# Splitting the bias rows of a graph network's first layer, moving query rows to GpSimd, and a new instruction order for the first block

## The chip, the cores and the metric

One NeuronCore of a Trainium2 chip runs the whole kernel in one launch. The metric is the device time of one execution in microseconds (us); several runs are given by their median. The engines are TensorE (PE), VectorE (DVE), ScalarE (ACT), GpSimd (POOL) and SyncE (SP). Each works through its own instruction queue in order; an instruction waits for semaphores of other engines or of transfers (DMA).

## The reference, cut

Four graph layers run over 4096 nodes with 64 features and a 0/1 adjacency matrix `adj` of 4096 x 4096. The change touches only the first:

```python
h = relu(layernorm(x))
h = lorentz_linear(h, W, b, scale)        # x @ W.T + b, then a time column and a rescaled rest
q = lorentz_linear(h, Wq, bq, scale_q)
k = lorentz_linear(h, Wk, bk, scale_k)
att = sigmoid((2 + 2 * (qm @ k.T)) / att_scale + att_bias)   # qm: q with the time column negated
support = (adj * att) @ h
x = x + support / sqrt(|-support[:, 0]**2 + sum(support[:, 1:]**2)|)
# layers 2 to 4: a decayed sum over the last 100 neighbours, a sum A @ h, a mean over neighbours
```

`lorentz_linear` gives `time = sigmoid(h[:, 0]) * exp(scale) + 1.1` as the first column and `h[:, 1:] * sqrt((time**2 - 1) / sum(h[:, 1:]**2))` as the rest.

## The kernel before, in words

**Blocks and masks.** Nodes are 32 tiles of 128 rows, eight blocks of four tiles. For each block of 512 targets the adjacency comes in 16 pieces of 128 x 2 x 512 (`load_masks`, L226, a DMA on POOL's queue that turns f32 into fp8), 128 pieces in all, block 7 first. Eight semaphores serve these loads in turn, so a load waits until the one eight before it has landed. `todo` lists the pieces in order. The masks of four blocks (64 pieces) have room from the start; the other four share room with the prologue's tiles (`pro`), and are opened after `pro_stack.close()`.

**The prologue** (`first_rows_and_block`, `before0`) makes h, q and k for two groups of 16 tiles, tiles 16 to 31 first. For each group: layer norm on DVE and ACT (`st`, `xc`, `sq`, `va`, `rs`), transposes on PE (`pt_h`), copies by ACT (`ht`), a product with W (`ps_h`; L719 adds the bias by a product of `ones` with `brow`, L727 multiplies by the weights), copies by ACT (`t`), the sigmoid and squares (`sgh`, `sqh`), sums and roots on DVE (`rrh`, `t2h`), the rows `fb` on DVE with their time column on POOL (L854); then the same for queries and keys together: `pt_q`, `hq`, `ps_q`, `tq`, `sqq`, `rrq`. Keys (`kr`) are made by DVE, with the time column by POOL (L903). Queries go to `s2a` (the same room as `q_sb`; L892, L903): those of tiles 16 to 31 by DVE, those of tiles 0 to 15 by POOL. Keys are transposed (`pt_k`) and laid by ACT as `kt`, queries of a block (`pq`, L989) as `qt`.

**Bias rows.** `bias_rows` (L501 to L510, POOL) splits the three bias vectors, 192 columns, into three bf16 parts that add up, and puts them into rows 0 to 2 of each half of `brow`. Twelve POOL operations do it.

**The first block.** The scores of block 7 (`ps`, L1053) need `kt` and `qt`; ACT takes the sigmoid into `att`, DVE multiplies by the mask, and PE gathers with `fb` (`acc`, L1084). Six `att` tiles and three score places rotate. All steps of prologue, block 7 and two pieces of block 6 are parts of a `Listing`, each with an engine and a planned time; `run` emits them by the list of numbers `ORDER`, taking the first part that can go. The first 40 mask loads are parts too. While PE has nothing planned, `fill` puts in products of `ones` (`idle`, L1178), 43 at the start and then planned idle time divided by 0.215.

**The loop.** The other pieces go in rounds of up to four: scores, sigmoid, mask, one mask load each (`load_masks(1)`), then gathers of the round before. `queries(ib - 1)` transposes the next block's queries, `rows0` finishes a block's rows (POOL's `sup`, `rs_a` and others). From the 33rd piece on, DVE also checks pieces of the adjacency (`ck`, loaded by SP).

The functions that the diff touches:

Of the kernel before, what the change touches and what calls it, by code (L numbers as in the profile page):

```python
# [24 lines left out]
D = 64  # L25
P = 128
# [17 lines left out]


ORDER = (
    206, 207, 205, 209, 208, 203, 210, 0, 1, 2, 3, 5, 4, 7, 9, 6, 8, 10, 213, 64, 11, 12, 14, 15,
    204, 13, 16, 18, 17, 211, 216, 65, 66, 67, 68, 69, 70, 19, 71, 217, 20, 21, 72, 214, 73, 127,
    74, 75, 76, 22, 79, 24, 23, 212, 215, 26, 218, 77, 78, 81, 25, 27, 28, 219, 80, 83, 82, 84,
    29, 31, 30, 85, 87, 33, 34, 32, 86, 221, 89, 88, 35, 36, 220, 37, 38, 90, 91, 222, 39, 40, 92,  # L50
    41, 43, 93, 94, 45, 96, 95, 97, 44, 223, 98, 47, 49, 100, 224, 46, 225, 42, 99, 102, 48, 101,
    50, 51, 52, 53, 60, 103, 104, 106, 56, 108, 110, 54, 57, 128, 105, 55, 61, 107, 129, 109, 111,
    62, 133, 228, 63, 161, 112, 113, 134, 149, 226, 114, 162, 230, 121, 115, 130, 150, 145, 146,
    163, 157, 151, 116, 131, 153, 119, 137, 138, 123, 124, 232, 135, 132, 164, 152, 120, 139, 158,
    136, 122, 154, 169, 147, 233, 173, 155, 170, 177, 174, 229, 165, 117, 231, 234, 156, 166, 58,
    59, 148, 159, 160, 167, 118, 235, 178, 140, 179, 236, 237, 125, 141, 126, 189, 193, 171, 142,
    143, 181, 238, 190, 185, 239, 172, 186, 191, 192, 144, 175, 176, 187, 241, 194, 195, 200, 182,
    201, 197, 240, 180, 198, 183, 184, 202, 242, 199, 196, 188, 227, 168,
)


# [32 lines left out]
def kernel(  # L94
# [87 lines left out]
    def model(general):  # L182
# [7 lines left out]
        def pool(name, bufs, on=stack, **kw):  # L190
            return on.enter_context(tc.tile_pool(name=name + sfx, bufs=bufs, **kw))
# [284 lines left out]
        pro = pool("pro", 1, pro_stack, side="right")  # L476
        pa0 = pool("pa0", 1, l0, space=PSUM)
        pps = [pool(f"pp{n}", 1, l0, space=PSUM) for n in range(2)]
        ppro = pool("pp_p", 1, pro_stack, space=PSUM)
        w_sb = pro.tile([P, NW], F32, name="w_sb" + sfx)  # L480
        weights_in(w_sb)
        for gr in range(1, len(ROWS)):
# [7 lines left out]
        ones = pro.tile([P, P], BF16, name="ones" + sfx)  # L490
        dve.memset(ones, 1.0)

        def bias_rows():
            v = vec[:, V_B : V_B + 3 * D]
            sel = pro.tile([P, 3], F32, name="sel" + sfx)
            high = pro.tile([P, 3 * D], BF16, name="high" + sfx)
            left, part = (
                pro.tile([P, 3 * D], F32, name=f"brow_{a}{sfx}") for a in ("left", "part")
            )
            total = pro.tile([P, 3 * D], F32, name="brow_sum" + sfx)  # L500
            nc.gpsimd.tensor_tensor(sel, ident[:, 0:3], ident[:, D : D + 3], ALU.add)  # L501
            for n in range(3):
                nc.gpsimd.tensor_copy(high, v if n == 0 else left)
                to = total if n == 0 else part
                nc.gpsimd.tensor_scalar(to, high, sel[:, n : n + 1], None, ALU.mult)
                if n:
                    nc.gpsimd.tensor_tensor(total, total, part, ALU.add)
                if n < 2:
                    nc.gpsimd.tensor_tensor(left, v if n == 0 else left, high, ALU.subtract)
            nc.gpsimd.tensor_copy(brow, total)  # L510

        class Listing:

# [10 lines left out]
            def add(self, engine, us, emit, *after, takes=(), frees=None, at=0.0, form=None):  # L524
                part = SimpleNamespace(
                    engine=engine, us=us, emit=emit, after=after, takes=takes, frees=frees, at=at,
                    form=form, n=len(self.parts), then=[], place=None,
                )
                for q in after:
                    q.then.append(part)  # L530
                self.parts.append(part)
                return part
# [49 lines left out]
                dve.scalar_tensor_tensor(q, q, share, a, ALU.mult, ALU.mult)  # L582
                dve.tensor_tensor(to, q, z, ALU.add)

        tables, flats = [], []

        TURN = ("pm", "pa")

# [1 line left out]
            on, tag = (pm, "pr") if part.place == "pm" else (pa0, "pa")  # L590
            return on.tile(list(shape), F32, tag=tag, name=name + sfx)

        def before0(todo, gr, bias):

            v = SimpleNamespace(at={})
            r0, R = ROWS[gr]
# [4 lines left out]
            def add(engine, us, emit, *after, **kw):  # L601
                return todo.add(engine, us, emit, *after, **kw)
# [132 lines left out]
            for u in HALF:  # L735
                pairs = [(k, k) for k in range(u * HK, (u + 1) * HK)]
                hs.append(
                    add(
                        "PE", 1.3 if u == 0 else 1.05, product("ht", pairs, 1, W_L, u == 0, "h"), ht[u], *hs, bias,
                        **({"takes": ("ps", "pp1")} if u == 0 else {}),  # L740
                    )
                )
# [123 lines left out]

            def q_out(u):
                def emit(_):
                    if u == 0:
                        v.tq = buffer("C", "tq", [P, len(HALF), 2, 2 * HK, D])  # L870
                    act.copy(v.tq[:, u].rearrange("p s k d -> p s (k d)"), v.at[f"q{u}"])
                return emit

            for u in HALF:
                pairs = [(k, u * HK + k) for k in range(HK)]
                qs.append(
                    add(
                        "PE", 1.3, product("hq", pairs, 2, W_QK, True, f"q{u}"), hq[u],
                        takes=("ps", "pp1"),
                    )  # L880
                )
                tq.append(add("ACT", 1.02, q_out(u), qs[u], frees=qs[u]))
# [29 lines left out]
                kr.append(add("DVE", 0.65, qk_rows(u, 1, nc.vector), rq, *kr))  # L912
                krw.append(add("POOL", 0.3, qk_times(u, 1), kr[u]))
            for u in reversed(HALF):
                if lead:
                    q = add("DVE", 0.65, qk_rows(u, 0, nc.vector), rq)
                else:
                    q = add("POOL", 1.35, qk_rows(u, 0, nc.gpsimd), rq)
                fq[u] = add("POOL", 0.3, qk_times(u, 0), q)
            ktd = across(lambda u: v.kr[:, of(u), :], "k", [[x] for x in krw], None)  # L920
            return hw, fq, ktd

# [166 lines left out]
        def first_rows_and_block():  # L1089
# [1 line left out]

            listing = Listing()
            add = listing.add
            bias = add("POOL", 8.1, lambda _: bias_rows(), at=6.5)
            made = [before0(listing, gr, bias) for gr in range(len(ROWS))]

            table = add("ACT", 1.5, lambda _: act.activation(tried, tried, AF.Sigmoid), *tables)
            for part in flats:
# [88 lines left out]

        with tc.manual_schedule():
            acc, late = first_rows_and_block()
            push(rows0(order0[0], evacuated(order0[0], acc, 0)), 10)  # L1190
            pro_stack.close()
            mp1 = pool("mask_b", 1, side="right")
            for ib in order0[EARLY:]:
                get_mask(mp1, ib)
            pps.append(pool("pp2", 1, l0, space=PSUM))
            if not general:
                push(count_constants(), 1)
            asking = iter(())

            def on():  # L1200
                step()
                next(asking, None)

            sizes = [2] * 8 if general else [4] * 4
            first = [2] * 7 if general else [4, 4, 3, 3]
            sizes = first + (NIB - 2) * sizes + [0]
            k, done = NG + 2, NG
            LEAVING = {112 - 4 * ib: ib for ib in range(NIB)}  # L1210
            for size in sizes:
                now = []
                for n, (ib, g) in enumerate(todo[k : k + size]):
                    edge[0] = n == size - 1
                    ps = scores(ib, g)

                    if size > 2 and not now:
                        att = frm = sigmoids(ps, att_tile(ib, g))
                    else:
                        frm, att = sigmoids(ps), att_tile(ib, g)  # L1220
                    masked(ib, g, frm, att)
                    now.append((ib, g, att))
                    load_masks(1)
                    k += 1
                    if k == 92 and not general:
                        push(count_constants_2(), 1)
                    if not general and k in LEAVING:
                        taken(LEAVING[k])
                    if k > 2 * NG and k % 8 in (0, 2, 4, 5, 7):
                        check()  # L1230
                    on()
                for ib, g, att in late:
                    at = done % NG
                    if at == 0:
                        acc = pa0.tile([P, IB], F32, tag="pa", name=f"acc0_{ib}{sfx}")
                        if ib > 0:
                            asking = queries(ib - 1)
                    gather(acc, fb, g, att, at)
                    if at == NG - 1:
                        push(rows0(ib, evacuated(ib, acc, 0)), 10)  # L1240
                    done += 1
                late = now
            edge[0] = True
            if len(checks) % 2:
                check()
            if general:
                drain()
# [659 lines left out]
```

## Time and profile before

| | us |
|---|---|
| median of 3 runs | 569.07 |
| lowest, highest | 568.34, 570.71 |
| the profiled execution | 568.73 |
| its span | 567.0 |
| PE busy | 544.4 |
| DVE busy | 468.2 |
| ACT busy | 357.1 |
| POOL busy | 280.2 |

The span runs from the first to the last instruction that the profile shows. PE's busy time holds its filler matmuls. The chain of waits follows the work that ended last back through what released it; in a line of it the first number is the start, the second the duration. In the windows each row is a stretch of time with the busy time of each engine (and the count of its instructions), the granted TensorE clock as a share of full speed, the share of time that the DMA engines were busy, and GB/s.

### The profile page before, as it was taken

What the parts mean: (1) busy time and instruction counts of PE and PEld (TensorE: products, weight loads), DVE (VectorE), ACT (ScalarE), POOL (GpSimd) and SP (SyncE); (2) the same over time, 40 slices, a digit from 0 to 9 for tenths busy, and PEclk for the clock granted to TensorE, in tenths of its full rate; (3) what the DMA queues carried; (4) which work ended last, traced back from release to release, by engine and by line L of the source; (5) the groups of instructions that cost most, each with busy time, mean ns of one, the idle gap of its engine ahead of it and who ended that gap; (6) DMA issues with size and microseconds to landing.
All of it is one profiled execution on the core that took longest, in us unless ns stands there. A gap on an engine that the chain in (4) does not pass through costs nothing.

```text
span 567.0 us, 9853 instructions
## 1 busy us (share of the span) xinstructions
PE 544.4 (96%) x3335; PEld 279.5 (49%) x3335; DVE 468.2 (83%) x949; ACT 357.1 (63%) x651; POOL 280.2 (49%) x538
## 2 busy tenths in 40 slices
PE   8898999999999999999999999999999999999995
PEld 3553333333333333332334445445454888888884
DVE  5788866899998999898965977778969897789992
ACT  3589577667766758778632888988888332342231
POOL 8626614666867575754345400475644442234332
PEclk9899999999999999999999999999999999999998
DMA  8983992798999999993234255443534778859960
GB/s 141 146 82 32 86 96 20 84 145 142 166 153 148 170 151 172 130 156 97 92 123 136 102 201 163 141 153 116 173 125 149 251 266 294 281 173 328 353 242 21
DMA packets 45612, 87.86 MB, mean 155 GB/s; under 512 B 6272, under 2 KB 24576, under 8 KB 45552
## 3 DMA queue, kind: packets, MB, share of 16 engines
q1 hardware_dynamic: 26112, 69.14, 36.3%
q0 software_dynamic: 18912, 17.77, 33.5%
q8 instruction: 28, 0.46, 0.3%
q10 hardware_dynamic: 528, 0.23, 0.2%
q14 instruction: 32, 0.26, 0.1%
HBM read 135.60 MB, written 1.05 MB: 241 GB/s over the span
## 4 chain that ended last, share of the span: by engine, by line
PE 63%; DVE 14%; POOL 8%; DMA 7%; ACT 4%; issue 3%; SPq 0%; ACTq 0%; DVEq 0%; POOLq 0%
PE acc L1627 15%; PE acc L1084 13%; PE ps L1053 12%; PE acc L1530 8%; PE cnt L1495 8%; DVE att L88 4%; DMA mask<-adjt_dram 3%; DVE ckw L88 2%; POOL mask L226 2%; PE many L1382 1%; DMA s2a<-adjt_dram 1%; DVE s2a L88 1%; PE idle L1178 1%; DMA vec<-vecs_dram 1%; ACT w L88 1%
## 5 line engine op out<-in xcount | busy, mean ns | idle before, releaser
L1053 PE MATMUL ps<-qt,kt 64*128 64x512 f32 x512 | 122.3, 608 | 3.6 <-DVE att L88 3.3
L1084 PE MATMUL acc<-att,fb 128*64 128x512 f32 x512 | 117.1, 599 | 0.5 <-DVE att L88 0.5
L1627 PE MATMUL acc<-s,mask 128*128 128x256 f16 x1024 | 114.0, 273 | 0.4 <-DVE s L88 0.4
L88 ACT ACTIVATE w<-cnt 128x512 int16<-128x512 f32 x187 | 98.7, 606 | 13.0 <-PE cnt L1495 12.1
L1627 PEld LDWEIGHTS <-mask 128*128 128x128 fp8e4 x1024 | 99.8, 98 | 12.9 <-issue 1.0
L88 DVE TENSOR_TENSOR att<-ps,mask 128x1024 f32<-128x1024 f32 x82 | 98.6, 1218 | 9.1 <-ACT ps L88 8.9
L88 DVE SCALAR_TENSOR_TENSOR ckw<-ckw 128x1024 f32<-128x1024 f32 x76 | 96.0, 1273 | 4.0 <-DMA ckw<-adjt_dram 4.0
L88 ACT ACTIVATE ps<-ps,att_c,att_a 128x1024 f32<-128x1024 f32 x82 | 93.8, 1176 | 1.1 <-PE ps L1053 0.7
L88 ACT ACTIVATE att<-ps,att_c,att_a 128x1024 f32<-128x1024 f32 x46 | 54.4, 1203 | 53.0 <-PE ps L1053 48.6
L1053 PEld LDWEIGHTS ps<-qt,kt 64*128 64x128 f32 x512 | 46.1, 186 | 77.5 <-issue 30.2
L226 POOL DMA_DIRECT2D mask<-adjt_dram x128 | 70.3, 562 | 11.0 <-DMA mask<-adjt_dram 9.5
L1495 PE MATMUL cnt<-mask,after 128*128 128x512 fp8e4 x256 | 67.4, 379 | 3.6 <-DMA mask<-two 1.3
L88 DVE TENSOR_TENSOR att<-att,mask 128x1024 f32<-128x1024 f32 x46 | 57.2, 1263 | 14.6 <-ACT att L88 11.2
L1084 PEld LDWEIGHTS acc<-att,fb 128*64 128x64 f32 x512 | 33.8, 136 | 71.6 <-issue 68.4
L1530 PE MATMUL acc<-w,s2a 128*128 128x512 bf16 x256 | 66.2, 379 | 1.2 <-ACT asb L88 1.2
L88 DVE TENSOR_SCALAR w<-cnt 128x512 int16<-128x512 f32 x69 | 46.9, 686 | 23.2 <-PE cnt L1495 22.6
L316 POOL TENSOR_TENSOR rs_a<-rs_y 128x4 f32<-128x4 f32 x48 | 19.1, 398 | 67.6 <-DVE rs_y L88 61.1
L88 DVE SCALAR_TENSOR_TENSOR ck<-ck 128x512 f32<-128x512 f32 x60 | 42.8, 714 | 0.8 <-DMA ck<-adjt_dram 0.8
L1530 PEld LDWEIGHTS <-s2a 128*128 128x128 f16 x256 | 24.7, 98 | 33.6 <-issue 5.6
L88 ACT ACTIVATE xm<-xm,inn 128x64 f32<-128x64 f32 x32 | 10.4, 347 | 47.3 <-DVE high L88 45.1
L1495 PEld LDWEIGHTS <-after 128*128 128x128 bf16 x256 | 24.5, 99 | 31.8 <-issue 2.7
L88 DVE SCALAR_TENSOR_TENSOR s2a<-s2a 128x1024 f32<-128x1024 f32 x22 | 27.7, 1268 | 1.8 <-DMA s2a<-adjt_dram 1.8
(248 smaller groups left out, 611.3 us busy)
## 6 DMA issues: line engine op xcount, KB each, us to landing
ckw<-adjt_dram SPq DMA_DIRECT2D x76, 512.0 KB, 4.4
mask<-adjt_dram POOLq DMA_DIRECT2D x128, 128.0 KB, 8.6
ck<-adjt_dram SPq DMA_DIRECT2D x60, 256.0 KB, 6.0
s2a<-adjt_dram SPq DMA_DIRECT2D x22, 512.0 KB, 4.9
x_sb<-x_dram SPq DMA_DIRECT2D x4, 256.0 KB, 7.5
out_dram<-y POOLq DMA_DIRECT2D x15, 64.0 KB, 3.7
apart_m<-mask SPq DMA_DIRECT2D x16, 16.0 KB, 4.5
mask<-apart_m SPq DMA_DIRECT2D x16, 16.0 KB, 4.7
```

Of the source, the lines that this page charges most:

```text
L88: return op(out, *args, **kw)
L226: nc.gpsimd.dma_start(out=masks[ib][:, g * CG : (g + 1) * CG, :], in_=adjt[ib, g])
L316: nc.gpsimd.tensor_tensor(a, y, y, ALU.mult)
L1053: nc.tensor.matmul(ps[:, c, :], kt[half, g, :], qts[ib][half, :], start=True, stop=True)
L1084: nc.tensor.matmul(acc[c * D : (c + 1) * D, :], lhs[:, t, :], rhs[:, c, :], start=(at == 0), stop=(at == NG - 1), skip_group_check=True,)
L1178: nc.tensor.matmul(v.idle[:, v.filling % CG, :], ones, ones.unsqueeze(1).to_broadcast([P, IB // P, P]), start=True, stop=True, skip_group_ ...
L1382: nc.tensor.matmul(pc[q * NT : (q + 1) * NT, :], lane[:, NT - 1 - t : 2 * NT - 1 - t], masks[quad * QUAD + q][:, t, :], start=(t == 0), st ...
L1495: nc.tensor.matmul(cnt, by, what, start=True, stop=True, skip_group_check=True)
L1530: nc.tensor.matmul(accs[ib], apart_s if t < 0 else both(s2a, t), w, start=(t == NT - 1), stop=False, skip_group_check=True,)
L1627: nc.tensor.matmul(acc[:, to, :, :].rearrange("p k d -> p (k d)"), masks[ib][:, t, c * P : (c + 1) * P], s23[:, t, :, :].rearrange("p k d ...
```

## The change

1. `bias_rows` takes a range of columns. The first 64 (for the product with W) are made first, as a part of its own planned at 3.8 us; the other 128 (for queries and keys) are a second part planned at 6.2 us, on which the products `ps_q` now depend. In the new order POOL issues eight mask loads before the first part (seven before the single one until now) and five between the parts.
2. Blocks 7 and 6 need only the queries of tiles 24 to 31. DVE makes these as before. The other three sets of eight tiles are put into `queries_left`, and POOL makes one (a product and a time write) after each of the first three mask loads of the loop.
3. The prologue's room is given back, and the tiles of the later masks opened, after the last of those; the score place of the prologue is given back before the loop, as before.
4. `ORDER` is a new list. By it PE gets 11, 7, 5, 10, 2, 13 and 1 fillers where it had 14, 5, 5, 10, 2, 13 and 1 (after the 43 at the start). DVE masks seven pieces before its second product `kr` of the second group (six before), and ACT does the last `sqq` before its second copy to `kt` (after it before).

```diff
 ORDER = (
-    206, 207, 205, 209, 208, 203, 210, 0, 1, 2, 3, 5, 4, 7, 9, 6, 8, 10, 213, 64, 11, 12, 14, 15,
...
+    202, 201, 204, 199, 203, 200, 205, 198, 0, 2, 3, 4, 6, 8, 208, 5, 7, 10, 9, 207, 63, 206, 209,
...
-        ppro = pool("pp_p", 1, pro_stack, space=PSUM)
+        ps_stack = ExitStack()
+        ppro = pool("pp_p", 1, ps_stack, space=PSUM)
...
-        def bias_rows():
-            v = vec[:, V_B : V_B + 3 * D]
-            sel = pro.tile([P, 3], F32, name="sel" + sfx)
-            high = pro.tile([P, 3 * D], BF16, name="high" + sfx)
+        sel = pro.tile([P, 3], F32, name="sel" + sfx)
+
+        def bias_rows(c0, n):
+            cols = slice(c0, c0 + n)
+            v = vec[:, V_B + c0 : V_B + c0 + n]
+            high = pro.tile([P, n], BF16, name=f"high{c0}{sfx}")
...
-            nc.gpsimd.tensor_tensor(sel, ident[:, 0:3], ident[:, D : D + 3], ALU.add)
+            if c0 == 0:
+                nc.gpsimd.tensor_tensor(sel, ident[:, 0:3], ident[:, D : D + 3], ALU.add)
...
-            nc.gpsimd.tensor_copy(brow, total)
+            nc.gpsimd.tensor_copy(brow[:, cols], total)
...
-        tables, flats = [], []
+        tables, flats, queries_left = [], [], deque()
...
-                        "PE", 1.3 if u == 0 else 1.05, product("ht", pairs, 1, W_L, u == 0, "h"), ht[u], *hs, bias,
+                        "PE", 1.3 if u == 0 else 1.05, product("ht", pairs, 1, W_L, u == 0, "h"), ht[u], *hs, bias_h,
...
-                        "PE", 1.3, product("hq", pairs, 2, W_QK, True, f"q{u}"), hq[u],
+                        "PE", 1.3, product("hq", pairs, 2, W_QK, True, f"q{u}"), hq[u], bias_qk,
...
             for u in reversed(HALF):
-                if lead:
+                if lead and u == HALF[-1]:
                     q = add("DVE", 0.65, qk_rows(u, 0, nc.vector), rq)
+                    fq[u] = add("POOL", 0.3, qk_times(u, 0), q)
                 else:
-                    q = add("POOL", 1.35, qk_rows(u, 0, nc.gpsimd), rq)
-                fq[u] = add("POOL", 0.3, qk_times(u, 0), q)
+                    queries_left.append((qk_rows(u, 0, nc.gpsimd), qk_times(u, 0)))
...
-            bias = add("POOL", 8.1, lambda _: bias_rows(), at=6.5)
-            made = [before0(listing, gr, bias) for gr in range(len(ROWS))]
+            bias_h = add("POOL", 3.8, lambda _: bias_rows(0, D), at=7.2)
+            bias_qk = add("POOL", 6.2, lambda _: bias_rows(D, 2 * D), at=7.2)
+            made = [before0(listing, gr, bias_h, bias_qk) for gr in range(len(ROWS))]
...
-            pro_stack.close()
-            mp1 = pool("mask_b", 1, side="right")
-            for ib in order0[EARLY:]:
-                get_mask(mp1, ib)
+            ps_stack.close()
             pps.append(pool("pp2", 1, l0, space=PSUM))
...
                     load_masks(1)
                     k += 1
+                    if queries_left:
+                        for emit in queries_left.popleft():
+                            emit(None)
+                        if not queries_left:
+                            pro_stack.close()
+                            mp1 = pool("mask_b", 1, side="right")
+                            for later_ib in order0[EARLY:]:
+                                get_mask(mp1, later_ib)
```

## The prediction

> **What bounds the kernel now.** I read the page first, then the chain of waits over the first 60 us, then the engines' timelines and short windows there, since all that the change moves lies in that stretch or just behind it.
>
> ```profile
> span 567.0 us, 9853 instructions
> PE 544.4 (96%) x3335; PEld 279.5 (49%) x3335; DVE 468.2 (83%) x949; ACT 357.1 (63%) x651; POOL 280.2 (49%) x538
> ```
>
> TensorE (PE) is busy 96% of the span, but in the first 45 us much of that is filler (the `idle` matmuls). Real work of the attention layer begins with the scores at 44.88. In windows from 56.76 to 77.00 PE has no gap, and from 77 to 107 one of 0.21 us. So a gain is worth what it moves the moment from which PE is full of scores and gathers; later work shifts with it.
>
> The chain of waits, cut to the stretch from 0 to 60 us (start, duration, what), gives the way there:
>
> ```profile
> 0.79 6.43 DMA vec<-vecs_dram
> ...
> 15.35 0.70 POOL brow L510
> 16.05 0.04 issue
> 16.09 0.39 PE ps_h L719 x2
> 16.48 1.88 PE ps_h L727 x32
> 18.37 4.61 PE idle L1178 x14
> 22.98 0.87 PE pt_h L678 x8
> ```
>
> The biases land at 7.22; GpSimd (POOL) works on all 192 columns of their rows until 16.05, and PE's first product waits for that. Then the chain runs through 14 filler matmuls: the normalised rows are ready at 21.3, but PE reaches their transposes only at 22.82. The windows show why the fillers are slow (columns: PE, PEld, DVE, ACT, POOL busy, then the granted clock, DMA share, GB/s):
>
> ```profile
> 17.00:18.00 1.00, 1.00 (x22) 1.00 (x20) 0.91 (x2) 0.25 (x1) 1.00 (x3) 0.97 1.09 258
> 18.00:19.00 1.00, 1.00 (x6) 0.46 (x5) 0.00 (x0) 0.60 (x2) 1.00 (x3) 0.50 1.08 252
> 20.00:21.00 1.00, 1.00 (x4) 0.42 (x3) 1.00 (x2) 0.99 (x2) 0.53 (x1) 0.50 1.06 107
> ```
>
> The granted clock is 0.50 from 18 to 21, after a hole (12.36 to 16.09) in which PE did only 1.17 us of transposes.
>
> From 50 us on VectorE (DVE) leads. POOL's timeline there:
>
> ```profile
> 49.94 1.55 POOL L892 TENSOR_TENSOR s2a<-tq,rrq 128x512 f32<-128x512 f32 x1 [4.97 <-ACT att L88]
> 52.64 1.98 POOL L892 TENSOR_TENSOR s2a<-tq,rrq 128x512 f32<-128x512 f32 x1
> ```
>
> and the windows beside it:
>
> ```profile
> 50.00:52.72 2.72, 2.11 (x10) 0.57 (x8) 2.72 (x3) 2.66 (x6) 2.72 (x3) 1.00 0.01 3
> 52.72:56.76 4.04, 3.53 (x17) 1.10 (x17) 4.04 (x4) 3.48 (x4) 4.01 (x4) 1.00 0.20 14
> 56.76:64.60 7.84, 7.84 (x40) 2.97 (x38) 6.52 (x8) 4.60 (x4) 6.48 (x13) 1.00 0.95 79
> ```
>
> DVE has no pause from 50.00 to 56.76, and PE lacks 0.61 and 0.51 us there. Of the maskings (`att<-att,mask`, 1.21 us each) the two that start beside these POOL products, at 50.50 and 53.63, took 2.07. The chain names a mask transfer landing at 50.13 as releaser of the first; DVE was busy with `kr` until 50.50 anyway, so I don't count it.
>
> **The change, step by step.** All against the profiled execution, 568.73 us (span 567.0 and 1.73 around it), 0.34 below the median of 569.07.
>
> *1. Bias rows of 64 columns first.* The same 11 operations took 8.77 us (7.28 to 16.05) at 192 columns. A POOL product of 128x4 takes 0.20, so 11 of them with gaps of 0.06 bound it at 2.9 from below, the old 8.8 from above. A product of 192 columns takes 0.54, which gives 0.31 at 64; casts and scalings by the same share make about 4.5: ready at 11.8. PE ends the transposes at 14.75, so any cost under 7.5 is hidden. The first product begins at 14.78 instead of 16.09, ends near 17.1 instead of 18.37. ScalarE (ACT) is busy with `sq` until 17.25, so its copies `t` move from 18.40 to 17.25: 1.15 gained there.
>
> *2. Fillers 11 instead of 14, later 7 instead of 5.* In other places 13 take 2.98 and 10 take 2.33, 0.23 each. At full clock the 11 end at 19.65. DVE, freed 1.15 earlier by ACT's `rs`, has the second half of `xc` ready at 20.15, PE transposes it until 20.7. ACT finishes `sqh` at 21.2 (22.35 less 1.15) and copies `ht` from there instead of from 23.89. PE's 7 fillers end at 22.3, bias products 0.35, and the first `ps_h` product of the second group starts at 22.65 instead of 25.26: 2.6 gained. That needs the full clock. The hole in PE's matmuls shrinks to 12.36 to 14.78, and in the 3 us before 17.95 PE gets 1.3 us more work than before, so I take it; with 0.50 the fillers end at 21.0, the transposes at 22.05, the product at 24.05: 1.2 gained.
> The Trainium skill ("TensorE: Matmul & The Clock Gate", What's actually happening) says that half rate follows an idle window of some 3.4 us, on windows that run free of the kernel. The old hole is 3.7 us and the trace agrees; the new one of 2.4 can't hold such a window, so by that rule the 2.6 stands.
>
> *3. The other 128 columns, on POOL.* Before them stand five mask loads, each waiting for the landing of the load eight before it; the fifth of those landed at 4.2 + 11.9 = 16.1, so the work starts near 16.9. At 128 columns it costs between 2.9 and 8.8; 6.5 by columns gives 23.4. Four more loads of 0.55 follow (the one they wait for last landed at 16.6 + 6.6 = 23.2), to 25.6, and then `fb`'s time copies, 0.4 each, which PE's transposes `pt_q` want at 26.4. It is hidden by 0.4 only; at 8.8 the copies come 2.3 later (first at 28.3) and eat most of step 2. The products that need these columns start after the transposes and are safe.
>
> *4. To the first scores.* From `pt_q` to `kr` order and counts stay, so all shifts by 2.6; a load put between `fb`'s two last copies delays a half that is needed 0.5 us later: nothing. Scores begin at 42.3.
>
> *5. DVE's busy stretch.* ACT does the last `sqq` before a copy of `kt`: DVE's last reduction, which waited for it until 46.39, comes 0.5 earlier. The two POOL products leave this stretch (2 x 0.86 on DVE), `kr`'s time is written by POOL at once instead of behind a 1.55 product, and one `s2a` product of 0.68 leaves DVE. That outweighs what PE lacked, 0.61 + 0.51 = 1.12, which caps the gain; seven maskings now precede DVE's second `kr`, and gathers of 0.92 follow maskings of 1.21, so some 0.2 stays: 0.9 gained, 0 to 1.12.
>
> *6. Queries in the first round.* Three POOL products with their three time writes now stand behind the 41st, 42nd and 43rd mask load, beside the last maskings of block 7. By landings of 1.25 us each that is about 65 to 73. Queued behind them are mask loads needed 20 tiles later and `sup` of block 7 (88.13 less 3, POOL having been idle 11.6 us before it). PE's transposes of block 5's queries wait for the first product; they stood at 88.82, 13 us later: hidden. Beside DVE each product costs a masking 0.86, together 2.6; DVE's idle times between 61.4 and 77.0 are 1.32, 0.73, 1.04 and 0.64, together 3.7, and PE leads there. Between 0 and 2.6 I take 0.3, near the lower end since the idle time exceeds the cost.
>
> *7. Pools.* The later masks' tiles are opened after the third query; their first load is the 65th, some 20 tiles on. Nothing.
>
> Sum: 2.6 + 0.9 - 0.3 = 3.2; 568.73 - 3.2 = 565.5, on the medians 565.9.
>
> **The rivals.**
> *Half clock stays* (25%): the early gain is 1.2; 1.2 + 0.9 - 0.3 = 1.8, 567.3. For it: the drop came only at 17.95, when PE had worked again for 1.9 us, so the short hole may do it too. Against: more work ahead of that point.
> *POOL late with the second bias rows* (10%): `pt_q` at 28.3 instead of 28.91, 0.6 + 0.9 - 0.3 = 1.2, 567.9. For it: scalings beside DVE took 1.59 and 1.77 against 0.77. Against: loads were issued at 0.55 steadily.
> *The new order gives nothing* (8%): the order was laid out on planned costs (1.25 for a masking, none for shared access); if other waits take the place of those removed, 569.1.
> *GpSimd's queries hold DVE* (12%, slower): if DVE stands still for each whole triple, product and time write (1.98 + 1.20 as the longest seen), that is 9.5 us; less the 3.7 idle, PE loses 5.8, and 3.5 - 5.8 = -2.3: 571.4, and 573 with half clock too. It decides above 3.7 + 3.5 = 7.2 us, 2.4 per query. For it: 2.07 against 1.21. Against: that was 0.86 per product, and maskings that read PSUM follow soon.
> The Trainium skill ("SBUF — State Buffer", Who interferes with whom) states such a lock: a DVE operation with two SBUF inputs and a GpSimd operation that reads SBUF exclude each other for a whole instruction. By that rule the masking of 50.50 would end at 51.49 + 1.21 = 52.70; it ended at 52.57, so the trace agrees for one instruction.
>
> **How the numbers follow.** The forecast has 45%. Low end: 2.7 + 1.12 = 3.8 makes 565.3, less 0.7 for scatter (runs lay 0.7 below and 1.6 above the median) and 0.3 for rounding: 564.3. High end: no gain and most of the upper scatter, 570.5. That leaves the slow rival out. A measurement of this kernel tells about 0.5% (2.85 us) from no change: below 566.2 is faster, above 571.9 slower. The forecast lies 0.3 under the first line, so about 0.37 of its 0.45 counts as faster, with 0.05 from scatter of the others; the slow rival and scatter give 0.09; 0.49 is left.
>
> **What would show it.** `ps_h` right after the transposes near 14.8; granted clock 1.00 from 18 to 21 (if not, the first rival); first scores near 42.3; maskings of 1.21 at the start, PE without gaps in the 12 us behind the scores; the three POOL products at 65 to 73 with PE still full. It is wrong if `pt_q` waits for `fb` on POOL, if PE waits for maskings between 60 and 75, or if the later stages (layer two from about 292 on) do not move by the same amount.

## The result, and the profile after

The changed kernel takes 565.69 us (median of 13 runs, 564.68 to 566.08), the kernel before in the same comparison 567.29 (13 runs, 566.16 to 571.14): a ratio of 0.9953 with an interval of 0.9936 to 0.997. The profiled execution after took 565.22 us, with a span of 563.4; the one before took 568.73, with 567.0. The new time lies 0.2 below the forecast; the gain in this comparison is 1.6 us, 1.25 short of the 2.85 that the prediction asked of a clear change.

The page's first lines after:

```profile
span 563.4 us, 9870 instructions
PE 544.1 (97%) x3334; PEld 278.8 (49%) x3334; DVE 469.1 (83%) x948; ACT 357.1 (63%) x651; POOL 281.7 (50%) x550
```

TensorE does the same work (544.1 against 544.4 us) in a span 3.6 us shorter. The chain of waits (start, duration, what) now runs through the first stage like this:

```profile
13.92 0.88 PE pt_h L681 x8
14.80 0.32 PE ps_h L722 x2
15.13 1.97 PE ps_h L730 x32
17.10 2.48 PE idle L1182 x11
...
19.58 1.23 PE pt_h L681 x8
20.81 1.51 PE idle L1182 x7
22.32 0.32 PE ps_h L722 x2
22.64 0.86 PE ps_h L730 x16
```

No bias operation is left in it: the product follows the transposes without a wait. The 11 fillers take 2.48 us where the 14 took 4.61, and the second group's product stands at 22.64. The windows of the same stretch (busy time of PE, PEld, DVE, ACT, POOL, then the granted clock, DMA share, GB/s) have the full clock:

```profile
16.00:18.00 2.00, 2.00 (x25) 1.46 (x24) 1.51 (x3) 1.74 (x4) 1.32 (x3) 1.00 1.11 202
18.00:20.00 2.00, 1.99 (x12) 0.90 (x9) 1.51 (x3) 1.97 (x6) 1.83 (x4) 1.00 1.10 203
20.00:22.00 2.00, 2.00 (x13) 1.07 (x11) 1.80 (x6) 2.00 (x5) 1.75 (x5) 1.00 1.11 151
```

The queries of GpSimd (POOL) in its timeline, and the windows of VectorE's (DVE's) busy stretch and of theirs:

```profile
63.23 1.07 POOL L895 TENSOR_TENSOR s2a<-tq,rrq 128x512 f32<-128x512 f32 x1
...
66.07 1.36 POOL L895 TENSOR_TENSOR s2a<-tq,rrq 128x512 f32<-128x512 f32 x1
...
69.19 1.37 POOL L895 TENSOR_TENSOR s2a<-tq,rrq 128x512 f32<-128x512 f32 x1
```

```profile
50.00:54.00 4.00, 4.00 (x22) 1.62 (x22) 4.00 (x5) 3.97 (x5) 1.99 (x4) 1.00 0.85 70
54.00:62.00 8.00, 8.00 (x38) 2.81 (x34) 5.17 (x6) 5.79 (x7) 4.50 (x9) 1.00 1.00 84
62.00:76.00 14.00, 13.71 (x62) 4.30 (x60) 13.20 (x9) 7.59 (x7) 10.34 (x12) 1.00 1.09 98
```

PE has no gap from 50 to 62, where it lacked 1.12 us before, and lacks 0.29 while the queries are made.

To follow a gain through the kernel I read five moments in every trace, in us from the span's start: the first `ps_h` product of the second group (A), the first `pt_q` transpose (B), the first scores (C), the transposes of block 5's queries (D), and the start of layer two (E, the first `many` product):

| kernel (profiled execution) | A | B | C | D | E | median, us |
|---|---|---|---|---|---|---|
| before | 25.09 | 28.91 | 44.88 | 88.82 | 292.19 | 567.29 |
| after | 22.48 | 26.30 | 42.87 | 86.13 | 289.16 | 565.69 |
| after, repeated | 22.49 | 26.30 | 42.87 | 85.85 | 288.79 | 566.01 |
| after, third time | 22.26 | 26.08 | 42.65 | 86.18 | 289.14 | 565.93 |
| bias rows in one part | 23.67 | 27.49 | 43.47 | 86.76 | 290.06 | 566.84 |
| split bias rows alone | 22.86 | 26.68 | 42.65 | 86.60 | 289.63 | 566.52 |
| queries early | 22.41 | 26.23 | 42.79 | 87.39 | 290.42 | 567.49 |
| queries made twice | 22.47 | 26.29 | 42.87 | 85.86 | 289.13 | 566.21 |
| before, hole filled | 23.92 | 27.74 | 43.71 | 87.67 | 290.69 | 567.38 |
| after, with a hole | 25.29 | 29.11 | 45.67 | 89.20 | 292.39 | 568.74 |
| after, fewer fillers | 21.44 | 25.71 | 42.33 | 85.63 | 288.64 | 567.71 |
| keys' times on VectorE | 22.59 | 26.41 | 42.48 | 85.56 | 288.65 | 565.05 |
| and the first queries' | 22.50 | 26.32 | 42.24 | 85.22 | 288.38 | 564.82 |

The median is D plus 479.5 to 480.4, with two exceptions: the kernel before (478.5), whose profiled execution was a longer one than its median, and the kernel with fewer fillers (482.1), told of below. The kernel with a hole lies in this range by chance: its profiled execution, 571.09, was the longest of its twelve. So the main question is what sets D.

### The profile page after: what moved, and what is told of

It reads as the page before. It is cut to its first block, busy times and chain, and to the rows that moved or that the text cites. A ratio compares the mean times of both kernels' runs of the same rounds, so it can differ in the third digit from the quotient of the medians.

```text
span 563.4 us, 9870 instructions
## 1 busy us (share of the span) xinstructions
PE 544.1 (97%) x3334; PEld 278.8 (49%) x3334; DVE 469.1 (83%) x948; ACT 357.1 (63%) x651; POOL 281.7 (50%) x550
## 4 chain that ended last, share of the span: by engine, by line
PE 66%; DVE 14%; ACT 6%; POOL 5%; issue 4%; DMA 3%; ACTq 0%; DVEq 0%; POOLq 0%; SPq 0%
PE acc L1636 15%; PE acc L1087 12%; PE ps L1056 12%; PE acc L1539 8%; PE cnt L1504 8%; DVE att L88 5%; PE idle L1182 3%; DVE ckw L88 2%; PE many L1391 1%; DVE s2a L88 1%; DMA s2a<-adjt_dram 1%; DMA mask<-adjt_dram 1%; ACT ps L88 1%; ACT w L88 1%; ACT att L88 1%
```

## The experiments

My theory had three parts: the biases that come first start the stage 1.2 us earlier (1); closing the hole in PE's work keeps the full clock (2); and moving GpSimd's queries out of DVE's busy stretch frees PE there (3). The main rival was that the queries, wherever they stand, hold DVE.

**The changed kernel again**, as control:

> The changed kernel as it stands, beside the three others on the same chip. Expected 564.7 to 566.1 us, ratio to before 0.993 to 0.997; granted clock 1.00 from 17 to 22 us; second group's first ps_h product at 22.5, first scores at 42.9, block 5's query transposes at 86.1.

Measured: 566.01 us (12 runs, 564.45 to 569.44), ratio 0.996 (0.9937 to 0.9983); D at 85.85, 0.28 earlier than in the first profile. Together with the third copy (B 0.22 earlier, D 0.05 later) that is the scatter of these moments.

**Bias rows in one part** again, all else as changed:

```
-            bias_h = add("POOL", 3.8, lambda _: bias_rows(0, D), at=7.2)
-            bias_qk = add("POOL", 6.2, lambda _: bias_rows(D, 2 * D), at=7.2)
+            bias_h = add("POOL", 3.8, lambda _: bias_rows(0, 3 * D), at=7.2)
+            bias_qk = add("POOL", 6.2, lambda _: None, at=7.2)
```

> The changed kernel with all 192 bias columns made in one go, as before; new order, 11 and 7 fillers and late queries stay. My theory (the early start of the first product carries the gain): brow ready at about 16, the second group's product 1.3 us later than in the changed kernel (23.8) if the clock stays full, 2.7 later if it falls to half; time 1.3 to 2.7 us above the changed kernel. Rival (the fewer fillers and the new order carry it): no more than 0.4 us above.

Measured: 566.84 us, ratio 0.998 (0.9962 to 0.9998). A and B are 1.2 later than after, as expected, at full clock; C is only 0.60 later, D 0.63 to 0.91, and the time 0.8, under the 1.3 expected. So half of what the split gains at B is given back before the scores. I come back to that. Two of the 12 executions have a mean granted clock under 0.9955, which matters for the hole below.

**The split alone**, in the kernel before; the second part of the rows stands behind the 12th mask load:

```
+            def first_bias():
+                bias_rows(0, D)
...
+            def one_load():
+                load_masks(1)
+                if loaded[0] == 12:
+                    bias_rows(D, 2 * D)
```

> The kernel before with the bias rows split alone (the other 128 columns after five more mask loads); old order, 14 and 5 fillers, queries as before. My theory: first product at 14.8, 14 fillers end at 20.3 at full clock, second group's product at 22.9 against 25.1: 2.2 us gained of the 2.6; block 5's query transposes at 86.6 against 88.8; time 2.2 us under before. Rival (the order carries it): under 1 us gained.

Measured: 566.52 us, ratio 0.9969 (0.9952 to 0.9986); A at 22.86, D at 86.60, at full clock. The moments came as expected, the time did not: 2.2 us under before were expected, and the medians differ by 1.2 (567.69 in this comparison), because the expectation started from a profiled execution that was longer than the median. That is still most of the gain, without the new place of the queries: from 50 to 54 PE still lacks 1.00 us.

**Queries early**: the changed kernel with all three queries put right behind the first time write of the second group's keys on GpSimd, into DVE's busy stretch (the room of the later masks is then opened before the loop again):

```
+            def keys_timed(u):
+                def emit(_):
+                    qk_times(u, 1)(_)
+                    if not lead and u == 0:
+                        while queries_left:
+                            for left in queries_left.popleft():
+                                left(None)
+                return emit
...
-                krw.append(add("POOL", 0.3, qk_times(u, 1), kr[u]))
+                krw.append(add("POOL", 0.3, keys_timed(u), kr[u]))
```

> The changed kernel with the three query products and time writes on GpSimd put back into the prologue, right behind the first key time write of the second group. My theory: they stand beside the first maskings again, two or three of which take 2.07 us, and PE lacks 0.6 to 1.1 us between 50 and 62; time 0.5 to 1.1 us above the changed kernel. Rival (PE has slack there, the products' place is indifferent): within 0.3 us.

Measured: 567.49 us, ratio 0.9987 (0.9971 to 1.0004). C is as after, D 1.2 to 1.5 later than in the three copies of it, the time 1.5, more than the theory had. The windows of this run show where:

```profile
50.00:54.00 4.00, 3.94 (x22) 1.25 (x20) 4.00 (x4) 3.97 (x5) 3.91 (x3) 1.00 0.00 0
54.00:58.00 4.00, 3.09 (x16) 1.03 (x14) 4.00 (x3) 0.48 (x2) 3.82 (x4) 1.00 0.02 4
58.00:62.00 4.00, 3.49 (x19) 1.29 (x16) 2.26 (x3) 4.00 (x4) 4.00 (x8) 1.00 0.55 43
```

PE lacks 0.06 + 0.91 + 0.51 = 1.48 us, and its waits name both causes (longest of each last):

```profile
PE acc L1096 <- DVE att L88: 0.9, 1, 0.9
PE pt_k L681 <- POOL kr L906: 0.5, 1, 0.5
```

The gather waits for a masking, and the keys' transpose for their last time write, which this place puts behind the queries on GpSimd. So the place of the queries is worth 1.2 to 1.5 us, and 0.5 of it is that write and not a slowed VectorE.

**Queries made twice**, in their new place (each is computed a second time, with the same values):

```
-                        for emit in queries_left.popleft():
+                        for emit in 2 * queries_left.popleft():
```

> The changed kernel with each of the three late query products and time writes done twice on GpSimd (the same values written again). My theory: DVE's idle time covers them, PE full from 62 to 85 but for 0.5 us; time within 0.5 us of the changed kernel. Rival (GpSimd's queries hold DVE): three more products cost what three cost, 0.86 us of DVE each or more, 2.6 us on PE: 568.3.

Measured: 566.21 us, ratio 0.997 (0.995 to 0.9989); D at 85.86. The trace has six products on POOL's timeline, two of the longer ones here:

```profile
62.55 1.49 POOL L895 TENSOR_TENSOR s2a<-tq,rrq 128x512 f32<-128x512 f32 x1
...
65.30 1.86 POOL L895 TENSOR_TENSOR s2a<-tq,rrq 128x512 f32<-128x512 f32 x1
```

and the list of PE's waits from 47 to 88 is empty. Three more queries with their time writes cost nothing at D (85.85 to 86.18 in the three copies), and by the medians 0.2 to 0.5 us, in a comparison whose kernel before was itself 0.3 higher (568.02 against 567.69 and 567.74). The rival's 2.6 us are out for this place: GpSimd does slow single maskings (1.39 on average from 48 to 76, 1.21 undisturbed), but PE has scores ahead of them.

**The hole filled, in the kernel before** (5 more fillers at the start, 5 between the transposes and the first product; its edit is shown), and **the hole made again, in the changed one** (the 43 at the start become 34, nothing else):

```
+                v.parts = getattr(v, "parts", 0) + 1
+                planned = int((part.idle - 0.1) / 0.215) if v.filling else 48
+                for _ in range(5 if v.parts == 3 else planned):
```

> The kernel before with 48 instead of 43 fillers at the start and 5 more between the first group's transposes and its product, so that PE has no hole from 12 to 16 us; nothing else. Clock theory: granted clock 1.00 from 18 to 21, the 14 fillers end at 21.5 instead of 22.8, second group's product at 23.8 against 25.1: 1.3 us gained against the profiled execution of before, and the runs lie closer together. Rival (the half clock does not hang on the hole): no gain, clock 0.50 there as before.

> The changed kernel with 34 instead of 43 fillers at the start, so that PE does only transposes and small products from about 10.5 to 17 us. Clock theory: the clock falls to 0.50 for some 3 us between 14 and 21 in most executions, and the time is 0.7 to 1.5 us above the changed kernel. Rival (the small products keep the clock up, or the early gain does not hang on it): within 0.3 us.

Measured: filled 567.38 us (566.1 to 568.7), ratio 0.9987 (0.9968 to 1.0006), A 1.17 and D 1.15 earlier than in before's profile; with a hole 568.74 (567.02 to 571.09), ratio 1.0003 (0.9981 to 1.0025), A 2.8 and D 3.1 later than after's. The hole cost more than the 0.7 to 1.5 us expected: the time is 2.5 above that of the queries made twice, which ran in the same comparison. The windows with the hole:

```profile
12.00:14.00 2.00, 0.37 (x4) 0.40 (x4) 1.97 (x5) 0.31 (x1) 1.93 (x5) 1.00 1.14 126
14.00:16.00 2.00, 2.00 (x19) 1.54 (x19) 1.93 (x5) 1.43 (x3) 0.56 (x2) 0.77 1.14 155
16.00:18.00 2.00, 2.00 (x24) 2.00 (x22) 1.51 (x3) 0.88 (x2) 1.43 (x4) 0.50 1.12 201
```

and the stretch of the kernel before with the hole filled:

```profile
16.00:18.00 2.00, 2.00 (x31) 1.57 (x30) 1.55 (x3) 1.18 (x3) 2.00 (x5) 1.00 1.11 232
18.00:20.00 2.00, 2.00 (x18) 1.11 (x17) 0.11 (x1) 1.41 (x4) 1.71 (x4) 1.00 1.10 212
```

So the hole makes the half clock, and filling it takes it away. It doesn't do so in every execution. Each has a mean granted clock, and a few us at half rate show in it: of 99 timed executions of the kernel before in three comparisons, 40 have a mean under 0.9955, with a median of 569.50 us, and 59 lie above, with 567.13. The changed kernel and its two copies had none of 37 below, the filled one none of 12; the one with the hole 6 of 12 (569.96 against 567.76), and the one with the bias rows in one part, whose profile has a hole of 2.6 us, 2 of 12. That is why the profiled pair differs by 3.5 us and the medians by less: the profiled execution of before, with 0.994, was of the longer kind. The clock is not all that the hole costs: the six executions with the higher mean clock still lie 1.5 above the queries made twice. Up to 0.9 of that may be the late load that the next run shows; the rest stays open.

**Fewer fillers** in the changed kernel (2 instead of 7 and of 5, 10 instead of 11), since the second product waits only for the last filler:

```
+                planned = {11: 10, 7: 2, 5: 2}.get(planned, planned)
```

> The changed kernel with 10, 2 and 2 fillers where it has 11, 7 and 5. If the fillers now delay PE: the second group's product starts when ACT's ht is there (21.6 to 22.0 instead of 22.5), the queries' transposes at 25.9 when GpSimd's fb copies are done instead of 26.3; 0.3 to 0.5 us under the changed kernel. Rival: the clock falls to half in the gaps and the time is 0.5 us or more above.

Measured: 567.71 us, ratio 0.9994 (0.9974 to 1.0013). A is 1.04 earlier, C 0.54, as expected, and yet the time is not shorter, as the theory had it, but 1.5 longer than with the queries made twice, in the same comparison. Two things are seen. Half of the executions (6 of 12) have a mean clock under 0.9955 (568.13 against 567.20), as the rival had it, though not the profiled one, which was the fastest of the twelve (566.56). And in the profile the first mask row of layer two lands late. DVE's timeline in this run, and its PE wait:

```profile
293.51 1.23 DVE L88 SCALAR_TENSOR_TENSOR ckw<-ckw 128x1024 f32<-128x1024 f32 x1 [4.88 <-DMA ckw<-adjt_dram]
```

```profile
PE pw L1412 <- DVE wn_size L88: 1.0, 1, 1.0
```

and the same line of the changed kernel, repeated:

```profile
292.25 1.23 DVE L88 SCALAR_TENSOR_TENSOR ckw<-ckw 128x1024 f32<-128x1024 f32 x1 [3.47 <-DMA ckw<-adjt_dram]
```

The wait of 4.88 instead of 3.47 costs PE 1.0 us; the run with a hole has it too (4.79, PE 0.9), the eleven other traces don't (3.4 to 3.7). Why the load is late there, and whether it is so in every execution, stays open.

**Where the scores lost 0.6 us.** From B to C the kernel before needs 15.97 us, the changed one 16.57. In between, GpSimd writes the time column of the first keys, and PE's transposes wait for it. POOL and PE after:

```profile
39.71 0.75 POOL L906 TENSOR_SCALAR kr<-tmq 128x8 f32<-128x8 f32 x1 [5.05 <-ACT sqq L88]
```

```profile
40.52 0.66 PE L681 MATMUL pt_k<-ident,kr 128*128 128x128 f32 x4 [0.79 <-POOL kr L906]
```

and POOL before:

```profile
41.95 0.52 POOL L903 TENSOR_SCALAR kr<-tmq 128x8 f32<-128x8 f32 x1 [5.03 <-DVE kr L892]
```

DVE's product was done at 39.16 after and at 41.77 before; the write ended 1.31 and 0.70 behind it. In these two traces and in that of the bias rows in one part the write ends about 0.10 behind the end of a DVE operation beside it, as if it were let through only then; after, that is one DVE operation (0.6) later. The profile names ACT's `sqq` as what released the write after, and the write may have waited for that instead. So I gave the write to DVE, and in a second kernel that of the first queries as well, with the changed kernel as control:

```
-                krw.append(add("POOL", 0.3, qk_times(u, 1), kr[u]))
+                if lead and u == HALF[0]:
+                    krw.append(add("DVE", 0.2, qk_times(u, 1, nc.vector), kr[u]))
+                else:
+                    krw.append(add("POOL", 0.3, qk_times(u, 1), kr[u]))
...
-                    fq[u] = add("POOL", 0.3, qk_times(u, 0), q)
+                    fq[u] = add("DVE", 0.2, qk_times(u, 0, nc.vector), q)
```

(the last two lines in the second kernel only).

> The changed kernel once more, as the control for the two runs beside it: first scores at 42.9, queries of block 5 transposed at 85.9 to 86.1, time 565.7 to 566.2, and no execution with a mean granted clock under 0.9955 (none of 25 had one so far, while 25 of the 70 of the kernel before did, and those took 2.1 to 2.5 us longer).

> The time column of the first keys is written by VectorE right behind its product instead of by GpSimd. Theory: the 0.6 us that were lost between the first transposes for the queries (26.30) and the first scores (42.87) went into GpSimd's write, which came at 39.71 and ended at 40.46, 1.31 behind the product's end, where the kernel before had it 0.70 behind. Then the write takes VectorE 0.2, the keys are transposed at 39.5 to 39.8 instead of 40.52, the first scores come at 41.8 to 42.4, and block 5's queries at 85.1 to 85.6: 0.5 to 0.9 us less time than the control. Rival: the scores hang on the query copies on ScalarE or on the second half of the keys; then the scores move by at most 0.2 and the time not at all.

> As the run with the keys' time column on VectorE, and the time column of the first queries is written there too. If the queries' transposes are what the scores then wait for, another 0.2 to 0.4 us earlier than in that run (GpSimd's write behind VectorE's next product takes 0.6 to 0.7, VectorE's own 0.2); if it is the second half of the keys, whose product then stands 0.2 later, 0.2 later than in that run.

Measured: control 565.93 us, ratio 0.9967 (0.9944 to 0.9989); keys on DVE 565.05, 0.9947 (0.9927 to 0.9967); both 564.82, 0.9948 (0.9927 to 0.9968). The keys' transpose with the write on DVE, and the first scores with both writes there:

```profile
39.62 0.63 PE L681 MATMUL pt_k<-ident,kr 128*128 128x128 f32 x4
```

```profile
42.24 2.94 PE L1059 MATMUL ps<-qt,kt 64*128 64x512 f32 x12
```

B to C is 16.57 in the control, 16.07 and 15.92 in the two: 0.50 and 0.65 back, and B to D 0.95 and 1.20 shorter (60.10, 59.15, 58.90). The medians are 0.9 and 1.1 below the control. The theory holds, though the first scores with the keys alone came at 42.48, just outside its 41.8 to 42.4, in a profile whose B was 0.33 later than the control's. It was no wait for `sqq`: VectorE's write starts at 39.30, and the `sqq` operations beside it end at 39.85. The rival has a part: with the keys alone, the scores then wait 0.66 for the query copies on ScalarE. Both kernels are faster than the changed one by their medians, but the intervals against the kernel before overlap with the control's. Why the write misses its moment in the changed kernel and its variants, and not with the rows in one part (0.71 behind the product, with the same waits in front), stays open.

## Why the prediction was right, step by step

*Steps 1 and 2, the early stage* (2.6 at A): 25.09 to 22.48 in the profiles, 22.65 forecast for the product that began at 22.64. The bias rows were ready at 12.35, not 11.8, because two products of 64 columns beside DVE took 0.85 and 0.75 instead of 0.31. It lay under the cover, as planned. The step's own division, 1.2 with the clock at half and 2.6 at full, is what the hole experiments show: filling the hole in the kernel before gives 1.17 at A, the split another 1.06 there. The first rival, half clock, did not come. The forecast hole of 2.4 us was not there either in this profile, since the first fillers ended only at 13.92 (last section); holes of 2.2 and 2.4 us stand in the profiles with fewer fillers and with both writes on VectorE, and no half rate follows them there. The rule of the Trainium skill ("TensorE: Matmul & The Clock Gate", What's actually happening), half rate after an idle window of some 3.4 us in windows that run free of the kernel, agrees with the traces in part. Windows of 3.41 us can be read from them (last section), and the half rate followed holes of 3.7 us (before, 12.36 to 16.09) and 4.0 us (with a hole, 10.69 to 14.73); but no window was idle, for in the 3.41 us before the fall PE was busy for 2.06 us (before) and 1.46 (with a hole). So the prediction's "the trace agrees" said too much, and what fills a window enough to keep the clock stays open.

*Step 3, the other columns*: 17.10 to 23.36, forecast 16.9 to 23.4; loads to 25.5, `fb`'s copies at 25.49, forecast 25.6. Hidden, by little.

*Step 4, to the first scores*, is the term that was mis-sized: "all shifts by 2.6", to 42.3. Only 2.01 arrived, at 42.87. Counts and order did stay, but the time write on GpSimd slipped by 0.6 against the DVE operations beside it.

*Steps 5 and 6* (0.9 less 0.3): from C to D, 43.94 became 43.26, and 42.98 and 43.53 in the other two copies, 0.4 to 1.0 gained where 0.6 was forecast. The 1.12 that PE lacked is gone. The cost of the queries in the first round was 0.3 in the sum; doubling them shows none at D.

So 0.6 was lost at step 4, and what was won behind it lies between 0.2 less and 0.4 more than forecast; at D the profiles differ by 2.69, and by 2.97 and 2.64 with the other copies, for a sum of 3.2. The profiled times differ by 3.51; what is above 2.69 arose later in the kernel (3.03 at E), and the repeat alone differs from the first by 0.53 in time. That the forecast time was met within 0.2 us is in part luck: the 0.6 lost was made up by gains that the sum did not hold.

What the sum did not have is that the execution it started from was one of two kinds. Its base was the median of three runs, 569.07; thirteen runs gave 567.29. The forecast time holds because the time after has no second kind, and the gain in the comparison is 1.6 us instead of 3.2. Against the 59 executions of before at full clock (567.13) the 37 of the changed kernel (565.76) gain 1.4.

## What to carry to other kernels

Look first whether the profiled execution stands for the median: executions with a mean clock under 0.9955 took 2.4 us longer here, and a hole ahead of a stage that depends on TensorE's clock is worth closing even where it looks idle anyway. A gain at the head of a chain is worth what arrives at the point from which the main engine is full; a GpSimd write of 0.24 us between VectorE operations took half of one back, and VectorE did it sooner itself. Work for GpSimd cost next to nothing where TensorE led and up to 1.5 us where VectorE did, with the same instructions.

## What was not expected of the hardware

The clock fell to half not in the hole but behind it, 1.84 us after the first product had begun (before, at 17.93) and 0.36 after it (with a hole, at 15.09), and stayed there for 3.41 and 6.83 us of nearly unbroken matmuls. With a hole, PE was busy throughout from 15.09 to 18.50, and the full clock still came back only at 21.91.

The traces say more on this than the windows above. In all thirteen, every stretch of full or half clock between two changes is a whole multiple of 3.413 us: 1 and 2 (the two above at half), 4 and 3 (the full clock ahead of them), 159, 162 or 163 (the rest of the kernel). So the clock is set in steps of 3.41 us, and these begin at another place in each execution: the trace holds a granted clock only from 4.28 us on in before's profile and from 7.45 in after's. Until then the windows print 1.00, but a filler starts every 0.427 us, and from then on every 0.216. From 5 to 7 us, before and after:

```profile
5.00:7.00 2.00, 2.00 (x11) 0.88 (x9) 0.00 (x0) 0.00 (x0) 1.04 (x3) 1.00 1.05 205
```

```profile
5.00:7.00 2.00, 2.00 (x6) 0.73 (x5) 0.00 (x0) 0.00 (x0) 1.58 (x4) 1.00 0.98 194
```

So the first 43 fillers took 10.77 us in before's profile and 12.33 in after's, and the pause behind them varies by up to 1.6 us from execution to execution. Both profiles with a fall had an early start of the full clock (4.28 and 4.85); with the bias rows in one part it came at 6.75, the hole was 2.6 us, and the clock held. This may be why the clock falls in some executions only. No run sets the place of these steps at will, so it is not shown.
